# Storing ranks by halves, moving copies behind the first expert's weights, and reordering the join in a mixture-of-experts kernel

## The chip, the cores and the metric

The kernel runs on one core of one Trainium2 chip. The metric is the device time of one execution in microseconds, as the median of several runs. All data are 32-bit floats. In the text PE is TensorE, the matmul engine; DVE is VectorE, ACT is ScalarE, POOL is GpSimd and SP is SyncE, which here only issues DMAs.

## The reference

The input x holds 32 batches of 128 rows and 1024 columns. Two blocks are added to it, one after the other.

The first block mixes the 128 rows of each batch with a 128x128 matrix chosen by an index, and sends the 4096 rows that result through a mixture of 64 experts. Each row goes to its eight best experts; an expert takes at most 256 rows, in order, and rows beyond that are left out.

```
w = weights[cond]                                  # (32,128,128)
h = einsum('bct,bcd->bdt', x, w).reshape(4096, 1024)
probs = softmax(h @ gate_w.T);  w, sel = top_k(probs, 8);  w = w / w.sum()
pos  = running count of each expert's rows;  keep where pos < 256
out  = (silu(xin @ wg[e]) * (xin @ wu[e])) @ wd[e]   # xin: the 256 rows of expert e
x1   = x + sum over the 8 experts of w * out
```

The second block applies to each batch of x1 a linear map W with a low-rank correction (rank 16) of an adapter that the batch chooses, then a feed-forward map base_w with bias and a router that adds the low-rank maps of two of eight LoRA experts.

```
H   = x1 @ W.T + scal * (x1 @ A[adapter].T) @ Bm[adapter].T
y   = x1 + H @ base_w.T + base_b + 2 * sum over top-2 of gate * (H @ lora_A[e]) @ lora_B[e]
```

## The kernel before

The kernel has four stages on one core, one after the other. Times are those of the profiled execution.

Stage A, 0 to about 217 us, works on eight groups of four batches. For each group `scored` (L344) multiplies the transposed rows with the gate weights (products pxg; operands xTb and gw_sb), `logits` (L380) finds the eight best experts, and `mixed` (L362) mixes each batch (products ph) and stores the result h from ACT into the DRAM buffer `hbuf` (L373). `counted` (L410) makes two small products per half group: prk holds, for each expert and batch, the place of every row among the expert's rows and its weight. ACT copies both halves into one tile rk, and one DMA on ACT's queue stores it in the DRAM buffer `ranks` (L418). pcnt adds the counts to `upto`. `loaded_batch` (L332) loads x on SP six batches ahead. `carried` (L375) copies 512 KB of x from DRAM to the DRAM buffer `ybuf`, on SP's queue: the experts later add their outputs to ybuf. The loop over groups (L460 to L490) calls it for batch b - 8 from the ninth batch on, and the last eight copies follow the loop (L493 and L494). PE also works on products of the second block's weights meanwhile: `combined(0, d)` multiplies 388 columns of a head matrix with blocks of W (products pcw, tiles hw and WB_a), and stores them in the DRAM buffer `cwbuf`.

Between A and B, 217 to 277 us, the first search runs. `looked_up` (L214) works out on DVE in which batch each slot's row is, `fetched` (L235) gathers the rows of `ranks` for the first four experts with eight indirect DMAs on POOL (tile rkg, L242), and `found` (L253) compares and sums them on DVE (hit, byq) and multiplies byq with a constant on PE (product prow). `placed` writes the row numbers, and `gathered` (L299) fetches the rows of h on POOL (tile xin, L306). These steps are called between the halves of `combined(1, d)`: PE's order is eight products of a pcw, then prow, then the next eight.

Stage B, 277 to 2139 us, is a loop over the 64 experts. `loaded` (L555) issues the loads of wg, wu and wd on SP's queue, at 1.5 MB each. The tile of wg shares its two buffers with the head blocks hw, those of wu and wd share theirs with the blocks of W. At the end of each expert its outputs are added to ybuf by indirect DMAs on POOL (L704).

Stage C, 2139 to about 2203 us, joins the two blocks. The loop at L940 to L961 makes the last products of the head matrix, with nine steps d of eight products each (pcw<-hw,WB_b). `with_ones` (L768) adds the identity to a chunk of the map BM on DVE, for the new columns of step d. At d == 2 it does this for the other 640 columns of eight chunks, which come back from cwbuf, and `map_sums` (L750) forms four sums of them. At d == 3 `turned_x1` (L796) transposes the first pair of batches on DVE from xq into X; xq is loaded from ybuf by four DMAs on SP (`loaded_x1`, L774). At d == 4 `inner` (L805) multiplies X with the adapter maps (products px) and masks them (xm on DVE), and at d == 5 `turned_in` transposes xm on PE (products pt).

Stage D, 2203 to 2766 us, multiplies the 16 pairs of batches with the joined map (products pr_c) and stores the output.

What sets the order: the names dve, pe, act, pool and sync are wrappers (`InOrder`, L200) that keep the order of the program on their engine; all their instructions carry line L206 in the profile. Plain nc.sync and nc.gpsimd calls are placed by the scheduler. It lets an instruction pass another that waits for a buffer where no order is kept. [...]

The lines that matter for the wait of the last `ranks` store and for the join:

```
            act.dma_start(ranks[:, g * GB : (g + 1) * GB, :, :], rk_sb)
...
                if b >= 8:
                    carried(b - 8)
...
        if d == 2:
            for c in range(HC):
                with_ones(c, 0, first, BM[:, c, :, 0:first])
            map_sums(0, first)
        elif d == 3:
            X = turned_x1(0, xq, c1)
```

Of the kernel before, what the change touches and what calls it, by code (L numbers as in the profile page):

```python
# [8 lines left out]
F32 = mybir.dt.float32  # L9
# [8 lines left out]
P = 128  # L18
NB = 32
# [3 lines left out]
E = 64  # L23
# [9 lines left out]
GB = 4  # L33
# [18 lines left out]
def kernel(  # L52
# [31 lines left out]
    ybuf = dram.tile([NT + P, H], F32, name="ybuf")  # L84


    ranks = dram.tile([E, NB + 1, 2, P], F32, name="ranks")
# [38 lines left out]
    for q in range(1, NQ):  # L126
        nc.vector.tensor_scalar(over[:, q - 1 : q], pcol, float(q * Q), None, ALU.is_ge)
    nc.vector.tensor_reduce(quad, over, AX.X, ALU.add)
    inquad = const.tile([P, 1], F32, name="inquad")
# [70 lines left out]
    class InOrder:  # L200
# [7 lines left out]
    dve, pe, act, pool, sync = (  # L208
        InOrder(e) for e in (nc.vector, nc.tensor, nc.scalar, nc.gpsimd, nc.sync)
    )  # L210
# [3 lines left out]
    def looked_up(es):  # L214
# [5 lines left out]
        for j in range(NJ):  # L220
            past = fs.tile([P, n, NB], F32, name=f"past_{u}_{j}", tag="past")
            dve.tensor_scalar(past, some, slotc[:, j : j + 1], None, ALU.is_le)
            dve.tensor_reduce(batch[:, :, j], past, AX.X, ALU.add)
            dve.tensor_tensor(past, past, some, ALU.mult)
            dve.tensor_reduce(rank[:, :, j], past, AX.X, ALU.max)
            dve.tensor_scalar(
# [26 lines left out]
    def found(some, lo, hi):  # L253
# [9 lines left out]
        )  # L263
        dve.tensor_reduce(place, hit, AX.X, ALU.add)
        dve.tensor_tensor(
# [6 lines left out]
        mine = slice(u * NJ, u * NJ + n)  # L272
        dve.tensor_reduce(slot_w[:, mine], hit, AX.X, ALU.add)
        empty = fs.tile([P, n], F32, name=f"empty_{u}", tag="empty")
# [24 lines left out]
    def gathered(e):  # L299
# [15 lines left out]
            halves.append(xin)  # L315
        return halves


    with (
        tc.tile_pool(name="a1", bufs=1) as a1,  # L320
# [7 lines left out]
        def loaded_turned(b):  # L328
            xTs[b] = a6.tile([P, HC, P], F32, name=f"xTb_{b}", tag="xTb", bufs=4)
            sync.dma_start(xTs[b].rearrange("p j c -> p (j c)"), x_t[b])  # L330
# [41 lines left out]
                    dve.tensor_copy(h_sb[:, cols], ph)  # L372
            act.dma_start(hbuf[rows, :], h_sb)  # L373

        def carried(b):  # L375
            sync.dma_start(ybuf[b * P : (b + 1) * P, :], x[b])

        def logits(g, xg):  # L380
            plog = pa_sm.tile([P, GB, E], F32, name=f"plog_{g}", tag="sm")
            for t in range(GB):
                pe.matmul(plog[:, t, :], ws[g * GB + t], xg[:, t, :], start=True, stop=True)
            top = a2.tile([P, GB, K], F32, name=f"top_{g}", tag="top")
            left = a2.tile([P, GB, E], F32, name=f"left_{g}", tag="left")
            for t in range(GB):
                dve.max(top[:, t, :], plog[:, t, :])
                dve.match_replace(left[:, t, :], top[:, t, :], plog[:, t, :], LOW)
            nmax = a2.tile([P, GB], F32, name=f"nmax_{g}", tag="nmax")
            dve.tensor_scalar(nmax, top[:, :, 0], -1.0, None, ALU.mult)  # L390
            ex = a2.tile([P, GB, E], F32, name=f"ex_{g}", tag="ex")
            for t in range(GB):
                act.activation(ex[:, t, :], plog[:, t, :], AF.Exp, bias=nmax[:, t : t + 1])
            mask = a2.tile([P, GB, E], F32, name=f"mask_{g}", tag="mask")
            dve.tensor_scalar(mask, left, LOW, None, ALU.is_equal)
            return ex, mask

        def weights_of(g, ex, mask):
            wt = a2.tile([P, GB, E], F32, name=f"wt_{g}", tag="wt")
            dve.tensor_tensor(wt, ex, mask, ALU.mult)  # L400
            wsum = a2.tile([P, GB], F32, name=f"wsum_{g}", tag="wsum")
            dve.tensor_reduce(wsum, wt, AX.X, ALU.add)
            rsum = a2.tile([P, GB], F32, name=f"rsum_{g}", tag="rsum")
# [4 lines left out]


        def counted(g, mask, wt):  # L410
            rk_sb = a2.tile([E, GB, 2, P], F32, name=f"rk_{g}", tag="rk", bufs=1)
            for i in range(2):
                prk = pa_sm.tile([E, 2, 2, P], F32, name=f"prk_{g}_{i}", tag="sm")
                for t in range(2):
                    pe.matmul(prk[:, t, 0, :], mask[:, 2 * i + t, :], tri, start=True, stop=True)
                    pe.matmul(prk[:, t, 1, :], wt[:, 2 * i + t, :], ident, start=True, stop=True)
                act.copy(rk_sb[:, 2 * i : 2 * i + 2, :, :], prk)
            act.dma_start(ranks[:, g * GB : (g + 1) * GB, :, :], rk_sb)  # L418
            pcnt = pa_sm.tile([P, GB, E], F32, name=f"pcnt_{g}", tag="sm")
            pe.matmul(pcnt, ones, mask, start=True, stop=True)  # L420
            for t in range(GB):
                b = g * GB + t
                if b == 0:
                    dve.tensor_copy(upto[:, :, b], pcnt[:, t, :])
                else:
                    dve.tensor_tensor(upto[:, :, b], upto[:, :, b - 1], pcnt[:, t, :], ALU.add)
# [14 lines left out]
            yield  # L441

        gw_sb = a1.tile([P, HC, E], F32, name="gw_sb")
        loaded_turned(0)
        sync.dma_start(gw_sb.rearrange("p j e -> p (j e)"), gate_w)
        for b in range(1, GB):
            loaded_turned(b)
        for b in range(6):
# [13 lines left out]
        for g in range(NG):  # L462
            ex, mask = logits(g, xg)
            for t in range(GB):
                b = g * GB + t
                mixed(b)
                if t == 1:
                    wt = weights_of(g, ex, mask)
                if b + 6 < NB:
                    loaded_batch(b + 6)  # L470
                if b >= 8:
                    carried(b - 8)
            if g == NG - 2:
                for buf in (hbuf, ybuf):
                    act.dma_start(
                        buf[NT : NT + P, :].rearrange("p (n c) -> p n c", c=256),
                        zeros.unsqueeze(1).to_broadcast([P, H // 256, 256]),
                    )
                act.dma_start(ranks[:, NB, :, :], pad)
            for _ in range((0, 1, 1, 1, 1, 1, 2, 2)[g]):  # L480
                for _ in combined(*rest.pop(0)):
                    pass
            if g + 1 < NG:
                xg = scored(g + 1)
                if g == 0:
                    lefts += left_block("a", 1, "wd")
                    lefts += left_block("a", 2, "wu")
                if g == 4:
                    hws[1] = head_block(1)
            counted(g, mask, wt)  # L490
        part = {0: looked_up([0, 1, 2, 3])}
        fetched(part[0], 4 * NJ)
        for b in range(NB - 8, NB):  # L493
            carried(b)  # L494
        gathers = {}
        for d in range(HC + 1):
            step = combined(1, d)
# [38 lines left out]
    with (  # L536
# [18 lines left out]
        def loaded(e):  # L555
            wg_sb = wts.tile([P, HC * BW], F32, name=f"wg_{e}", tag="wg")
            nc.sync.dma_start(wg_sb[:, 0 : HC * I], wg[e])
            wg_sb = wg_sb[:, 0 : HC * I].rearrange("p (j i) -> p j i", j=HC)
            wu_sb = wts.tile([P, HC, I], F32, name=f"wu_{e}", tag="wu")
            nc.sync.dma_start(wu_sb.rearrange("p j i -> p (j i)"), wu[e])  # L560
            wd_sb = wts.tile([P, IC, H], F32, name=f"wd_{e}", tag="wd")
            nc.sync.dma_start(wd_sb.rearrange("p i h -> p (i h)"), wd[e])
            return wg_sb, wu_sb, wd_sb
# [160 lines left out]
    c1 = ctx.enter_context(tc.tile_pool(name="c1", bufs=1, reuse_waits="tile"))  # L724
# [71 lines left out]
    def turned_x1(q, xq, side):  # L796
        X = side.tile([P, KC, 2 * P], F32, name=f"X_{q}", tag="X", bufs=1)
        for t in range(2):
            dve.transpose(
                X[:, 0:HC, t * P : (t + 1) * P].rearrange("p j (q r) -> p q j r", r=Q),  # L800
                xq[:, t * NQ : (t + 1) * NQ, :].rearrange("p q (j c) -> p q j c", c=Q),
            )
        return X
# [131 lines left out]
    xq = loaded_x1(0, c1)  # L935
# [4 lines left out]
    for d in range(HC + 1):  # L940
        _, pcw = multiplied(2, d, hw, lefts, pc_p, "pp", pe)
        pcw = pcw.rearrange("p (n c) -> p n c", n=2)
        if d < HC:
            with_ones(d, first, 512, pcw)
        else:
            act.copy(BM[:, HC + 1, :, first:512], pcw)
        if d == 2:
            for c in range(HC):
                with_ones(c, 0, first, BM[:, c, :, 0:first])
            map_sums(0, first)  # L950
        elif d == 3:
            X = turned_x1(0, xq, c1)
        elif d == 4:
            pxs, xm = inner(0, X, ab)
            ab = own_maps(1)
        elif d == 5:
            turned_in(0, X, HC + 1, xm)
        elif d == 6:
            mid = routed(0, pxs, corrected(0, X, pxs))
        elif d == 7:  # L960
            turned_in(0, X, HC, mid)  # L961
# [8 lines left out]
    xq = loaded_x1(1, c3)  # L970

    for q in range(NQP):
# [21 lines left out]
        if more:  # L994
            X = turned_x1(q + 1, xq, side)
        if q + 2 < NQP:
            xq = loaded_x1(q + 2, (c1, c3)[q % 2])
# [99 lines left out]
```

## Time and profile before

| | |
|---|---|
| median of 3 runs | 2783.18 us (2773.07 to 2784.08) |
| the profiled execution, its own time | 2768.09 us |
| its span | 2766.4 us |
| PE busy | 2729.5 us, 99% of the span |
| DVE busy | 1581.5 us, 57% |
| POOL busy | 1123.1 us, 41% |
| ACT busy | 408.6 us, 15% |
| DMA | 585.11 MB, 212 GB/s in the mean |
| mean granted clock of TensorE | 0.992 |

PE's busy time by stage, from the windows view:

| stage | window, us | PE busy, us | clock | DMA busy |
|---|---|---|---|---|
| A | 0 to 217 | 204.85 | 0.95 | 96% |
| first search | 217 to 277 | 52.51 | 0.91 | 70% |
| B | 277 to 2139 | 1861.01 | | |
| C | 2139 to 2203 | 54.08 | 0.92 | 61% |
| D | 2203 to 2766.4 | 557.00 | | |

The page gives busy time per engine, then groups of instructions with the idle time ahead of them and what ended it. The list of waits gives, for one engine, the line, the operand that came last, the sum, the count and the longest wait. The timeline shows instructions in order of time; a bracket holds the idle time before one and its releaser. The windows view gives for a stretch the busy time of each engine, the granted clock (1.00 is full speed) and the share of time that the DMA engines were busy. All times count from the start of the span.

### The profile page before, as it was taken

The numbers are of one execution on the slowest core, as the hardware profiler recorded it, in microseconds if no ns is written. First come the engines' busy times: TensorE is split into PE (matmuls) and PEld (weight loads), VectorE is DVE, ScalarE is ACT, GpSimd is POOL, SyncE is SP. The second block draws the span as 40 slices with busy tenths as digits, with TensorE's granted clock in tenths as the row PEclk, the third lists the DMA queues.
The fourth block names the chain that finished last, engine by engine and source line by source line (L and its number), as shares of the span: only waits on it lengthen the run. The fifth ranks groups of instructions, "written<-read, shape, count | busy, mean of one in ns | idle before, by whom it ended". The sixth has DMA issues, their size and how long they took to land.

```text
span 2766.4 us, 23669 instructions
## 1 busy us (share of the span) xinstructions
PE 2729.5 (99%) x8580; PEld 1513.0 (55%) x8580; DVE 1581.5 (57%) x2521; ACT 408.6 (15%) x792; POOL 1123.1 (41%) x846
## 2 busy tenths in 40 slices
PE   8998999999999999999999999999999899999999
PEld 6765555555555555555555555555555555555554
DVE  2334667666676666766657667576563444444442
ACT  1220111111111111111111111111111000000000
POOL 2105365555655646556465564655451100000000
PEclk9999999999999999999999999999999999999999
DMA  9997777777878878777787777777775522222210
GB/s 349 381 376 263 238 255 227 248 262 225 251 241 243 255 225 252 256 234 248 235 249 254 229 247 253 241 244 238 237 248 153 137 74 62 62 61 65 60 43 38
DMA packets 131141, 585.11 MB, mean 212 GB/s; under 512 B 23312, under 2 KB 50000, under 8 KB 105168
## 3 DMA queue, kind: packets, MB, share of 16 engines
q1 hardware_dynamic: 71136, 405.18, 39.6%
q0 software_dynamic: 51200, 155.24, 24.3%
q10 hardware_dynamic: 8688, 23.17, 2.2%
q8 instruction: 68, 1.11, 0.2%
q14 instruction: 49, 0.40, 0.0%
HBM read 476.45 MB, written 123.83 MB: 217 GB/s over the span
## 4 chain that ended last, share of the span: by engine, by line
PE 96%; DMA 2%; DVE 1%; issue 0%; ACT 0%; SPq 0%; POOL 0%; ACTq 0%; DVEq 0%
PE pp L594 42%; PE po L693 23%; PE pr_c L206 17%; PE pcw L206 4%; PE px L206 2%; PE pxg L206 2%; PE ph L206 2%; PE pth L644 2%; DMA xTb<-in_x_t 1%; DMA hbuf<-h 1%; PE prk L206 1%; PE plog L206 0%; DMA rkg<-ranks,row 0%; PE pg L206 0%; PE pt L206 0%
## 5 line engine op out<-in xcount | busy, mean ns | idle before, releaser
L306 POOL DMA_INDIRECT xin<-hbuf,slot_row x512 | 722.6, 1411 | 159.2 <-issue 151.8
L693 PE MATMUL po<-wd,hTb 128*128 128x512 f32 x1536 | 680.3, 592 | 0.6 <-ACT hTb L646 0.6
L704 POOL DMA_INDIRECT ybuf<-o,slot_tok x128 | 205.3, 1604 | 666.1 <-ACT o L702 465.4
L693 PEld LDWEIGHTS po<-wd,hTb 128*128 128x128 f32 x1536 | 286.8, 190 | 323.7 <-issue 306.1
L594 PE MATMUL pp<-wg,xT 128*128 128x384 f32 x1024 | 351.6, 486 | 0.6 <-ACT G_sb L206 0.6
L594 PE MATMUL pp<-t,s 128*128 128x384 f32 x1024 | 341.9, 487 | 0.0
L594 PEld LDWEIGHTS pp<-t,s 128*128 128x128 f32 x1024 | 193.4, 190 | 141.9 <-issue 23.0
L206 DVE TENSOR_TENSOR u<-p,pp 128x384 f32<-128x384 f32 x64 | 35.4, 554 | 386.4 <-PE pp L594 386.4
L594 PEld LDWEIGHTS pp<-wg,xT 128*128 128x128 f32 x1024 | 189.6, 190 | 119.9 <-ACT G_sb L206 1.2
L702 ACT ACTIVATE o<-po,slot_w 128x512 f32<-128x512 f32 x256 | 175.9, 687 | 494.1 <-PE po L693 489.9
L206 POOL DMA_INDIRECT ab<-in_AT,adapter_rows x32 | 36.6, 1144 | 444.2 <-ACT pxw L206 438.9
L206 PE MATMUL pr_c<-BM,X 128*128 128x512 f32 x480 | 213.7, 592 | 0.0
L206 DVE STREAM_TRANSPOSE xT<-xin 128x1024 f32<-128x1024 f32 x128 | 156.1, 1235 | 67.6 <-DMA xin<-hbuf,slot_row 62.4
L594 PE MATMUL pp<-t,xT 128*128 128x384 f32 x512 | 175.6, 486 | 0.0
L594 PE MATMUL pp<-wu,xT 128*128 128x384 f32 x512 | 175.6, 486 | 0.0
L594 PE MATMUL pp<-wu,s 128*128 128x384 f32 x512 | 175.6, 486 | 0.0
L611 ACT ACTIVATE h<-gate 128x384 f32<-128x384 f32 x128 | 67.2, 525 | 699.6 <-DVE gate L206 699.6
L242 POOL DMA_INDIRECT rkg<-ranks,row x128 | 124.8, 975 | 96.7 <-DMA cwbuf<-cw 58.0
L206 PE MATMUL pr_c<-ts,ss 128*128 128x512 f32 x320 | 142.5, 592 | 1.3 <-DVE ss L206 1.3
L206 PEld LDWEIGHTS pr_c<-BM,X 128*128 128x128 f32 x480 | 88.9, 190 | 100.2 <-issue 100.0
L206 DVE TENSOR_TENSOR u<-u,pp 128x384 f32<-128x384 f32 x128 | 70.6, 551 | 125.0 <-PE pp L594 124.9
L594 PEld LDWEIGHTS pp<-wu,xT 128*128 128x128 f32 x512 | 97.3, 190 | 67.8
(158 smaller groups left out, 2920.4 us busy)
## 6 DMA issues: line engine op xcount, KB each, us to landing
wg<-in_wg SPq DMA_DIRECT2D x64, 1536.0 KB, 7.0
wu<-in_wu SPq DMA_DIRECT2D x64, 1536.0 KB, 9.7
wd<-in_wd SPq DMA_DIRECT2D x64, 1536.0 KB, 7.2
xTb<-in_x_t SPq DMA_DIRECT2D x32, 512.0 KB, 7.0
x<-in_x SPq DMA_DIRECT2D x32, 512.0 KB, 9.1
hbuf<-h ACTq DMA_DIRECT2D x32, 512.0 KB, 6.9
ybuf<-in_x SPq DMA_DIRECT2D x32, 512.0 KB, 8.3
xq<-ybuf SPq DMA_DIRECT2D x64, 256.0 KB, 5.1
```

The lines of the kernel that those rows point to most:

```text
L206: return lambda *args, **kw: kept(op(*args, **kw))
L242: nc.gpsimd.indirect_dma_start(out=some["rk"][:, s, :, :].rearrange("p i t -> p (i t)"), out_offset=None, in_=ranks.rearrange("e b i t -> ...
L306: nc.gpsimd.indirect_dma_start(out=xin[:, q, :], out_offset=None, in_=quarters, in_offset=bass.IndirectOffsetOnAxis(ap=slot_row[:, s : s + ...
L594: nc.tensor.matmul(bank, left[k][:, j, :], right[k][:, j, :], start=(j == 0), stop=(j == HH - 1))
L611: nc.scalar.activation(h, gate, AF.Sigmoid)
L644: nc.tensor.transpose(pt[:, i, :], h[:, i * P : (i + 1) * P], ident)
L693: nc.tensor.matmul(po, hT[j][:, i, :], wd_sb[:, i, cols], start=(i == 0), stop=(i == IC - 1),)
L702: nc.scalar.mul(o_sb[:, cols], po, slot_w[:, s : s + 1])
L704: nc.gpsimd.indirect_dma_start(out=ybuf, out_offset=bass.IndirectOffsetOnAxis(ap=slot_tok[:, s : s + 1], axis=0), in_=o_sb, in_offset=None ...
```

## The change

Five edits are made together.

- `counted` makes one tile per half group, and stores each half by its own DMA on ACT: sixteen stores of 128 KB in rows of 2 KB in place of eight of 256 KB in rows of 4 KB. The tile has two buffers instead of one.
- The load of gw_sb is issued ahead of the first xTb load instead of behind it.
- `carried` moves inside the condition on b + 6, so that the loop makes only copies 0 to 17.
- The other fourteen copies, 18 to 31, are issued in `loaded(0)`, between wu and wd of the first expert, and no longer in the loop and behind `fetched`. `carried` itself is defined further up so that it can be called there.
- In the join the two transposes of `turned_x1` are at d == 2, and the eight `with_ones` and `map_sums` at d == 3.

```diff
@@ -315,6 +315,9 @@
             halves.append(xin)
         return halves
 
+    def carried(b):
+        sync.dma_start(ybuf[b * P : (b + 1) * P, :], x[b])
+
 
     with (
         tc.tile_pool(name="a1", bufs=1) as a1,
@@ -372,9 +375,6 @@
                     dve.tensor_copy(h_sb[:, cols], ph)
             act.dma_start(hbuf[rows, :], h_sb)
 
-        def carried(b):
-            sync.dma_start(ybuf[b * P : (b + 1) * P, :], x[b])
-
 
 
         def logits(g, xg):
@@ -408,14 +408,15 @@
 
 
         def counted(g, mask, wt):
-            rk_sb = a2.tile([E, GB, 2, P], F32, name=f"rk_{g}", tag="rk", bufs=1)
             for i in range(2):
+                rk_sb = a2.tile([E, 2, 2, P], F32, name=f"rk_{g}_{i}", tag="rk")
                 prk = pa_sm.tile([E, 2, 2, P], F32, name=f"prk_{g}_{i}", tag="sm")
                 for t in range(2):
                     pe.matmul(prk[:, t, 0, :], mask[:, 2 * i + t, :], tri, start=True, stop=True)
                     pe.matmul(prk[:, t, 1, :], wt[:, 2 * i + t, :], ident, start=True, stop=True)
-                act.copy(rk_sb[:, 2 * i : 2 * i + 2, :, :], prk)
-            act.dma_start(ranks[:, g * GB : (g + 1) * GB, :, :], rk_sb)
+                act.copy(rk_sb, prk)
+                two = slice(g * GB + 2 * i, g * GB + 2 * i + 2)
+                act.dma_start(ranks[:, two, :, :], rk_sb)
             pcnt = pa_sm.tile([P, GB, E], F32, name=f"pcnt_{g}", tag="sm")
             pe.matmul(pcnt, ones, mask, start=True, stop=True)
             for t in range(GB):
@@ -441,8 +442,8 @@
             yield
 
         gw_sb = a1.tile([P, HC, E], F32, name="gw_sb")
+        sync.dma_start(gw_sb.rearrange("p j e -> p (j e)"), gate_w)
         loaded_turned(0)
-        sync.dma_start(gw_sb.rearrange("p j e -> p (j e)"), gate_w)
         for b in range(1, GB):
             loaded_turned(b)
         for b in range(6):
@@ -468,8 +469,8 @@
                     wt = weights_of(g, ex, mask)
                 if b + 6 < NB:
                     loaded_batch(b + 6)
-                if b >= 8:
-                    carried(b - 8)
+                    if b >= 8:
+                        carried(b - 8)
             if g == NG - 2:
                 for buf in (hbuf, ybuf):
                     act.dma_start(
@@ -490,8 +491,6 @@
             counted(g, mask, wt)
         part = {0: looked_up([0, 1, 2, 3])}
         fetched(part[0], 4 * NJ)
-        for b in range(NB - 8, NB):
-            carried(b)
         gathers = {}
         for d in range(HC + 1):
             step = combined(1, d)
@@ -558,6 +557,9 @@
             wg_sb = wg_sb[:, 0 : HC * I].rearrange("p (j i) -> p j i", j=HC)
             wu_sb = wts.tile([P, HC, I], F32, name=f"wu_{e}", tag="wu")
             nc.sync.dma_start(wu_sb.rearrange("p j i -> p (j i)"), wu[e])
+            if e == 0:
+                for b in range(NB - 14, NB):
+                    carried(b)
             wd_sb = wts.tile([P, IC, H], F32, name=f"wd_{e}", tag="wd")
             nc.sync.dma_start(wd_sb.rearrange("p i h -> p (i h)"), wd[e])
             return wg_sb, wu_sb, wd_sb
@@ -945,11 +947,11 @@
         else:
             act.copy(BM[:, HC + 1, :, first:512], pcw)
         if d == 2:
+            X = turned_x1(0, xq, c1)
+        elif d == 3:
             for c in range(HC):
                 with_ones(c, 0, first, BM[:, c, :, 0:first])
             map_sums(0, first)
-        elif d == 3:
-            X = turned_x1(0, xq, c1)
         elif d == 4:
             pxs, xm = inner(0, X, ab)
             ab = own_maps(1)
```

In the programs as built, PE's order of instructions is the same as before. On DVE only the join differs. On SP wu of the first expert goes ahead with eight of the fourteen copies, then wg, the other six copies and wd follow.

## The prediction

> **What bounds the kernel now.** I read the page first, then all waits of TensorE, then the timeline around each wait that the change touches, then the windows with the granted clock.
>
> ```profile
> PE 2729.5 (99%) x8580; PEld 1513.0 (55%) x8580; DVE 1581.5 (57%) x2521; ACT 408.6 (15%) x792; POOL 1123.1 (41%) x846
> ```
>
> TensorE is busy 2729.5 of 2766.4 us. The matmul order stays the same in the built programs, so only two things can be won: the 36.9 us in which PE idles, and the time it runs at half clock because of such idling. The list of PE's waits (total, count, longest) splits the idle time:
>
> ```profile
> PE px L206 <- issue: 9.9, 1, 9.9
> PE prow L206 <- DVE byq L206: 7.0, 1, 7.0
> PE pxg L206 <- DMA gw_sb<-in_gate_w: 6.5, 1, 6.5
> PE pxg L206 <- DMA xTb<-in_x_t: 3.4, 7, 1.4
> ```
>
> The change aims at the first three: the join (px), the first row search (prow) and the start (gw_sb). The prow chain in the timeline (start, busy, instruction, in brackets the idle time before it and its releaser):
>
> ```profile
> 218.27 0.58 ACT L206 COPY rk<-prk 64x512 f32<-64x512 f32 x1 [0.29 <-PE prk L206]
> 222.92 0.45 ACTq L206 DMA_DIRECT2D ranks<-rk  x1
> 226.91 0.95 POOL L242 DMA_INDIRECT rkg<-ranks,row  x1 [58.00 <-DMA cwbuf<-cw]
> ...
> 235.90 0.42 DVE L206 TENSOR_TENSOR hit<-rkg,rank 128x256 f32<-128x256 f32 x1 [12.78 <-DMA rkg<-ranks,row]
> ...
> 238.94 0.59 PE L206 MATMUL prow<-byq,spread 128*128 128x8 f32 x2 [7.04 <-DVE byq L206]
> 239.38 8.05 PE L206 MATMUL pcw<-hw,WB_a 128*128 128x388 f32 x16
> 247.41 5.46 PE L206 MATMUL pcw<-hw,WB_a 128*128 128x388 f32 x16
> ```
>
> The last ranks store is issued at 222.92, although its data is ready at 218.85: 4.07 us late. Each DMA of SP and ACT uses one of eight completion semaphores in turn and waits for the DMA that last used it. Here that was the hbuf store of 207.88, in flight for 15.0 us among the x copies (the three before it: 4.2 to 4.6). After prow, sixteen pcw take 8.05 us, later ones 5.46. The windows view says why (window, length, PE, PEld, DVE, ACT, POOL, clock, DMA, GB/s):
>
> ```profile
> 224.14:234.38 10.24, 7.75 (x24) 4.18 (x22) 0.00 (x0) 0.93 (x2) 5.69 (x6) 1.00 0.79 277
> 234.38:244.62 10.24, 5.68 (x10) 3.29 (x11) 5.99 (x21) 0.00 (x0) 5.54 (x6) 0.50 0.63 232
> 2169.73:2179.97 10.24, 4.64 (x18) 4.67 (x19) 7.12 (x7) 0.00 (x0) 0.00 (x0) 0.50 0.23 51
> ```
>
> An idle stretch is followed by 10.24 us at clock 0.50, here and at the join. Two more such spells stand at 60.30 and 186.59. The join in DVE's and PE's timeline:
>
> ```profile
> 2159.95 6.45 DVE L206 SCALAR_TENSOR_TENSOR BM<-chan,own,BM 128x640 f32<-128x640 f32 x8 [4.22 <-DMA BM<-cwbuf]
> ...
> 2173.46 0.61 DVE L206 SCALAR_TENSOR_TENSOR BM<-chan,own,pcw 128x384 f32<-128x384 f32 x1
> 2173.99 2.36 DVE L206 STREAM_TRANSPOSE X<-xq 128x1024 f32<-128x1024 f32 x2
> 2175.32 6.65 PE L206 MATMUL px<-pxw,X 128*128 128x152 f32 x32 [9.92 <-issue]
> ```
>
> and the last of the four loads of xq, which the transposes read (issued 2156.92, so landed 2170.2):
>
> ```profile
> L778 SPq DMA_DIRECT2D xq<-ybuf x1: 474/474/474, 2156.9 to 2156.9; - x1
> DMA to landing us min/median/max: 13.3/13.3/13.3
> ```
>
> "issue" hides that px waits for the transposes, and they behind 13.4 us of ones and sums on DVE (2159.95 to 2173.4).
>
> [...]
>
> **The change part by part.** All sums are against the profiled execution (span 2766.4 plus 1.69 around it, 2768.09), which is 15.1 us under the median of 2783.18; I move the median by the same amount.
>
> *gate_w first.* PE's first pxg needs gw_sb (landed 6.39) and xTb_0 (5.72). The same 768 KB go through one queue in either order. Cost 0, between -0.3 and +0.3: the 0.67 us between the landings, halved.
>
> *Ranks in halves, copies behind wu_0.* Eight more ACT issues of 0.45 us: ACT is busy 408.6 us in all, so they lie beside PE. In the built program SP runs on to wu_0 right behind copy 17 and the three small loads (about 193 us), then eight copies, then wg_0, six copies, wd_0: wg_0's buffer is released only by the first block's last product (216.3), so the scheduler lets wu_0 and eight copies pass. These are 5.5 MB between 193 and 216, where now fifteen copies (7.5 MB) are issued from 191 to 216. So the queue is nearly empty when the ranks come; the last half waits for the semaphore of the fourth copy, which waits for wu_0's landing (about 201) and lands near 210. The half is issued when its data is there, 219.1 instead of 222.92; behind it on ACT are only copies of later pcw, with four buffers between them and PE. But wg_0 (1.5 MB) and four copies (2 MB) start at 216.5: at about 400 GB/s (369 GB/s is the mean of 0 to 217 us, DMA 96% busy) they fill the queues to about 226.5, and the last two copies to 229. The half's landing takes 3.2 us (now, alone) to 7.6 (ranks of group 6 at 198.17, beside copies); I take 5: 224.1, gathers rkg from 224.9 (now 226.91). The second is issued at 226.2. Now the first two take 7.1 and 7.6 us beside wg_0 and wu_0; the shortest gathers in the trace take 2.6 to 2.8. I take its landing at 231.0, two us after the copies have drained; 3.3 us on through hit to prow (235.78 to 238.94 now, rounded up) gives 234.3. PE is ready at 231.9, so it waits 2.4 instead of 7.04: -4.6. [...] the half-clock spell still comes, and PE now has work in nearly all of it instead of 5.7 us; half of the extra 4.6 is lost: +2.3. Net **-2.3 us**. Bounds: -9.9 if the wait and the spell go (7.04 and half of 5.68; gathers at 2.8 us would do it); +0.4 with the half at 7.6 and the gathers at 7.6. Behind the waiting gathers on POOL only the xin gathers are queued, and their products have 8 us of slack: token sums end at 268.95, the first product is at 277.13.
>
> *Earlier groups.* Loop copies 18 to 23 leave a stretch that is DMA-bound, but only one xTb wait and no x wait sits there; 0, with 5.1 either way for a half-clock spell more or less (that is what those at 60 and 187 cost).
>
> *The join.* Two transposes move ahead of one pcw ones, eight ones and four sums. They can't start before xq lands at 2170.26; the change starts no xq load earlier. So DVE stands from 2155.7 to 2170.3[...]. PE: px from about 2171.5, at half clock to 2179.97, done about 2180.0; pcw 5 done 2185.3. DVE: 2170.3 + 2.3 (transposes) + 14.0 (3 x 0.6 less overlap, eight ones 6.45, four sums 7.2) = 2186.5, then 0.5 for with_ones(4): xm at 2187.0, its transposes on PE at 2187.75 against 2186.97 now: **+0.8 us**. The 9.9 us before px becomes about 6.1, and a new wait of 2.4 us stands behind pcw 5. That second gap may start another half-clock spell, up to +4.9 us; I take 0. The cover of the sums is gone: they lay beside the xq load.
>
> Sum: -2.3 + 0.8 = -1.5, 2766.6 for the profiled execution, **2781.7** for the median.
>
> **The rivals.**
> A. The join gains in full: xq lands by about 2160, say because the scatter adds or cwbuf drain earlier. Then px's 9.92 us and the 2.35 lost at half clock (6.65 against 4.30 for the same matmuls later) go: -12.3, with prow -2.3: -14.6, 2768.6. For it: DMA is idle enough after 2164. Against: 13.3 us to landing, queued behind BM's 2.5 MB. Chance 0.12. With C, -22.2 or 2761.0: 0.07.
> B. Slower: each group now holds two semaphores with ranks stores, and in the built program xTb_16/17, 20/21 and 24/25 wait on halves of groups 2 to 4; only xTb_17, 21 and 25 waited before. xTb_20 to 23 landed at 127.84 to 136.02 with PE needing them about 2 us apart, waiting 0.17 to 0.27 each: no reserve. A delay of half a microsecond per group plus a half-clock spell of 5.1 is 5.6; three groups give 16.8 - 1.5 = +15.3, 2798.5. It decides from three groups (two: 11.2 - 1.5 = +9.7, 2792.9, within the bound). Against: halves are stored earlier than the whole. Chance 0.10.
> C. The prow wait goes wholly, with its spell: -9.9 + 0.8 = -9.1, 2774.1. For it: 2 MB less ahead, and gathers of 2.8 us elsewhere. Against: wg_0 and six copies run beside the ranks and the gathers. Chance 0.15.
> D. The change doesn't do what its words say: wu_0 and eight of fourteen copies are ahead of wg_0; this is in the forecast.
>
> **How the numbers follow.** Forecast 0.56, A 0.12, A with C 0.07, B 0.10, C 0.15. A measurement of this kernel can tell about 0.5%, 13.9 us. Faster: A and A with C, with 0.01 for the tail of C, 0.20. Slower: B, 0.10. Same: 0.70. Range: low 2766.3, A with prow's full -4.6; high 2792.9, two groups of B. A with C and B stay outside, 0.17. The forecast's own range is 2774.1 (prow's lower bound) to 2789.3 (prow +0.4 instead of -2.3, and a spell in the second gap of the join, 4.9).
>
> **What the changed profile would show.** px waits about 6 instead of 9.9 us, DVE idle up to the transposes for xq, and pt (xm) 48.3 us after the join's first pcw (47.5 now); prow waits about 2.4 us; the last ranks half is issued near 219 and lands near 224, beside wg_0; four half-clock spells remain. I'm wrong if xq lands before 2165, if the last half is issued after 221 or prow doesn't wait, or if groups 4 to 6 show xTb waits of over half a microsecond.

## The result and the profile after

| | before | after |
|---|---|---|
| median of 22 runs each | 2783.31 us | 2788.77 us |
| ratio of after to before | | 1.0029, 95% interval 1.0016 to 1.0041 |
| the profiled execution: span | 2766.4 us | 2789.4 us |
| mean granted clock of TensorE | 0.992 | 0.988 |

The changed kernel is slower by 0.29%, about 8 us: the ratio is that of the means, which lie 8.0 us apart; the medians lie 5.5 us apart. That is less than the 0.5% that the prediction set as the bound of what can be told; 22 runs of each tell it. The two profiled executions differ by 23.0 us, since the one of before lies at the low end of its kernel's runs and the one of after close to its median. So where an argument rests on a size, several profiles are put side by side below. The 23.0 us lie in three places: 8.6 up to the end of stage A, 10.2 from there to the first product of the experts, and 4.2 from there to pg, the product that follows pt in the join. From pg to the end both take 574.0 us.

The list of PE's waits after the change (total, times, longest):

```profile
PE prow L206 <- DVE byq L206: 17.1, 2, 11.9
PE pxg L206 <- DMA xTb<-in_x_t: 11.3, 8, 6.5
PE px L206 <- issue: 7.2, 1, 7.2
PE pt L206 <- DVE xm L206: 4.1, 1, 4.1
```

The px wait has fallen from 9.9 to 7.2 us, and a wait for xm before pt has come in its place. The prow wait has grown from 7.0 to 17.1, in two waits of 11.9 and 5.2. The xTb wait now holds the 6.5 us of the start (gw_sb no longer lands last); the rest, 4.8 us, lies in the groups, where before had 3.4.

Beside the waits stands the clock. The granted clock in 1 us steps shows these half-clock spells. The last two columns give the end of PE's last product of stage A (prk) and the end of ACT's last copy to rk, which is called the end of stage A here:

| kernel | ranks stored | half-clock spells up to 205 us | sum, us | last product, us | end of stage A, us |
|---|---|---|---|---|---|
| before | whole, ACT | 60-71, 186-197 | 20.4 | 218.2 | 218.9 |
| before, second profile | whole, ACT | none | 0 | 210.1 | 210.7 |
| after | halves, ACT | 59-70, 110-124, 168-172, 199-203 | 30.7 | 223.5 | 227.4 |
| after, second profile | halves, ACT | 60-74, 115-126, 197-204 | 30.6 | 224.1 | 227.4 |

The start of group 4's operands in the timeline, before and then after (start, busy, instruction):

```profile
92.58 9.22 SPq L206 DMA_DIRECT2D xTb<-in_x_t  x4
94.14 0.46 ACTq L206 DMA_DIRECT2D ranks<-rk  x1
```

```profile
92.37 0.46 ACTq L206 DMA_DIRECT2D ranks<-rk  x1
93.48 0.45 ACTq L206 DMA_DIRECT2D ranks<-rk  x1
98.90 4.15 SPq L206 DMA_DIRECT2D xTb<-in_x_t  x4
...
108.92 2.49 PE L206 MATMUL pxg<-gw_sb,xTb 128*128 128x64 f32 x16 [0.70 <-DMA xTb<-in_x_t]
112.86 7.09 PE L206 MATMUL pxg<-gw_sb,xTb 128*128 128x64 f32 x32 [1.46 <-DMA xTb<-in_x_t]
```

Before, the first of the four xTb loads goes out at 92.58, ahead of the ranks store. After, it has to wait for the semaphore that the first ranks half holds (4.2 us in the list of SP's waits), and goes out at 98.90. PE then waits 0.70 us, and half clock begins at 110.3; the wait of 1.46 us falls into it. Behind that, 32 of these products take 7.09 us, where 64 took 7.25 at full clock.

Each DMA in a trace names its completion semaphore, so one can read which DMA used it last. In the trace of before the 465 DMAs of SP and ACT name eight of them, 58 or 59 DMAs each, and each of the 457 that use one again goes out after the DMA that used it last has landed: the xTb loads of 92.58 and 99.98 by 0.06 us, the ranks store of 222.92 by 0.07. The first xTb load of groups 4, 5 and 6, counted from 0:

| kernel | issued, us | its semaphore was last used by |
|---|---|---|
| before | 92.58, 118.83, 141.81 | a copy to ybuf |
| after | 98.90, 125.14, 150.65 | the first ranks half |
| halves alone, ACT | 98.77, 123.24, 149.29 | the first ranks half |
| halves alone, POOL | 92.80, 116.58, 140.67 | a load of x |
| quarters, ACT | 102.27, 129.32, 156.29 | a load of x; the copy to ybuf just ahead of it on SP waits for a ranks store |

The second load of these groups waits for a ranks store before the change too (99.98 for group 4).

The prow chain after the change:

```profile
223.15 0.38 PE L206 MATMUL prk<-ident,wt 128*64 128x128 f32 x2
223.37 0.58 ACT L206 COPY rk<-prk 64x512 f32<-64x512 f32 x1
226.35 0.45 ACTq L206 DMA_DIRECT2D ranks<-rk  x1
226.84 0.58 ACT L206 COPY rk<-prk 64x512 f32<-64x512 f32 x1 [2.90 <-DMA hbuf<-h]
227.45 0.45 ACTq L206 DMA_DIRECT2D ranks<-rk  x1
240.34 0.94 POOL L242 DMA_INDIRECT rkg<-ranks,row  x1 [62.21 <-DMA ybuf<-in_x]
...
249.10 0.60 PE L206 MATMUL prow<-byq,spread 128*128 128x8 f32 x2 [11.90 <-DVE byq L206]
```

The last half goes out 0.03 us after its copy has ended (227.42), but that copy is itself late. The first half is ready at 223.95 and its store waits until 226.35 for the semaphore of the hbuf store of 220.44; the second copy stands behind it on ACT (the bracket: 2.90 us). From the last product to the last store it takes 3.9 us, against 4.7 before (217.85 + 0.38 to 222.92):

```profile
217.85 0.38 PE L206 MATMUL prk<-ident,wt 128*64 128x128 f32 x2
```

The gathers start only 12.9 us after the store: it is in flight beside wg_0 and the six copies behind it. And the join after the change, DVE and PE:

```profile
2189.76 2.37 DVE L206 STREAM_TRANSPOSE X<-xq 128x1024 f32<-128x1024 f32 x2 [15.51 <-DMA xq<-ybuf]
...
2192.55 6.45 DVE L206 SCALAR_TENSOR_TENSOR BM<-chan,own,BM 128x640 f32<-128x640 f32 x8
...
2206.57 0.42 DVE L206 TENSOR_TENSOR xm<-px,smask 128x256 f32<-128x256 f32 x1
```

```profile
2191.11 6.67 PE L206 MATMUL px<-pxw,X 128*128 128x152 f32 x32 [7.19 <-issue]
...
2207.05 0.69 PE L206 MATMUL pt<-ident,xm 128*128 128x128 f32 x2 [4.11 <-DVE xm L206]
2207.53 7.97 PE L206 MATMUL pcw<-hw,WB_b 128*128 128x384 f32 x16
```

DVE stands 15.51 us until xq has landed, and only then makes the ones and sums. The sixteen pcw behind pt take 7.97 us instead of 5.33: a second half-clock spell.

### The profile page after: what moved, and what is told of

Same layout as the page of the kernel before. It is cut to its first block, busy times and chain, and to the rows that moved or that the text cites. A ratio compares the mean times of both kernels' runs of the same rounds, so it can differ in the third digit from the quotient of the medians.

```text
span 2789.4 us, 23677 instructions
## 1 busy us (share of the span) xinstructions
PE 2739.2 (98%) x8580; PEld 1519.4 (54%) x8580; DVE 1580.3 (57%) x2521; ACT 408.1 (15%) x792; POOL 1119.4 (40%) x846
## 4 chain that ended last, share of the span: by engine, by line
PE 93%; DMA 4%; DVE 1%; issue 0%; POOL 0%; ACT 0%; SPq 0%; ACTq 0%; DVEq 0%
PE pp L596 41%; PE po L695 23%; PE pr_c L206 17%; PE pcw L206 3%; PE px L206 2%; PE pxg L206 2%; DMA xTb<-in_x_t 2%; PE pth L646 1%; PE ph L206 1%; DMA hbuf<-h 1%; PE prk L206 1%; DMA ybuf<-in_x 1%; DMA xq<-ybuf 0%; DMA ranks<-rk 0%; DMA cwbuf<-cw 0%
```

## The experiments

The ratios are to the kernel before, run on the same chip in the same rounds, each with its 95% interval. A diff is to the kernel before, or to the experiment that its text names.

**Each part alone.** The join alone:

```diff
         if d == 2:
+            X = turned_x1(0, xq, c1)
+        elif d == 3:
             for c in range(HC):
                 with_ones(c, 0, first, BM[:, c, :, 0:first])
             map_sums(0, first)
-        elif d == 3:
-            X = turned_x1(0, xq, c1)
```

> Only the reordering of the join is made (transposes at d == 2, ones and sums at d == 3). Theory 1 (the transposes still wait for xq, so the ones and sums lose the cover of that load): the px wait falls from 9.9 us by some 3, a new wait of about 4 us stands before pt of xm, and the kernel is 2 to 5 us slower than before (ratio 1.001 to 1.002). Rival (the join pays by itself, what is lost is lost at the first search and in the groups): 5 to 12 us faster, ratio 0.996 to 0.998.

Measured: 1.0007 (0.9984 to 1.0030), which can't tell either sign. In its profile px waits 6.5 us and pt 4.6; from the first product of the experts to pg of the join the kernel has lost 3.0 us against before. In after it is 4.2, in the second profile of after 2.2, with whole ranks (below) 3.9. So the join alone costs 2 to 4 us in four profiles, and the rival, a gain of 5 to 12, is out. (This stretch differs by up to 1.7 us between the profiles whose join is as before.)

The copies alone, fourteen of them behind wu of the first expert:

```diff
-                if b >= 8:
-                    carried(b - 8)
+                    if b >= 8:
+                        carried(b - 8)
...
-        for b in range(NB - 8, NB):
-            carried(b)
...
             nc.sync.dma_start(wu_sb.rearrange("p j i -> p (j i)"), wu[e])
+            if e == 0:
+                for b in range(NB - 14, NB):
+                    carried(b)
```

> Only the copies are moved (18 to 31 behind the first expert's wu); ranks are stored whole. Theory 1 (the copies behind wg_0 now run beside the last ranks store and the gathers, which crowds both): the prow waits sum to 12 to 18 us instead of 7.0, and the kernel is 4 to 10 us slower. Rival (the halves of the ranks are what delays, through the two completion semaphores they hold): no slower than before, prow waits under 7 us.

Measured: 1.0015 (0.9994 to 1.0036), prow wait 12.9 us. The time leaves it open whether the copies cost anything.

The halves alone:

```diff
-            rk_sb = a2.tile([E, GB, 2, P], F32, name=f"rk_{g}", tag="rk", bufs=1)
             for i in range(2):
+                rk_sb = a2.tile([E, 2, 2, P], F32, name=f"rk_{g}_{i}", tag="rk")
...
-                act.copy(rk_sb[:, 2 * i : 2 * i + 2, :, :], prk)
-            act.dma_start(ranks[:, g * GB : (g + 1) * GB, :, :], rk_sb)
+                act.copy(rk_sb, prk)
+                two = slice(g * GB + 2 * i, g * GB + 2 * i + 2)
+                act.dma_start(ranks[:, two, :, :], rk_sb)
```

> Only the ranks are stored by halves. Theory 1 (the copies are at fault): within 2 us of before, prow wait near 7 us, xTb waits as before. Rival (halves hold two semaphores and delay the xTb loads of groups 4 to 6): xTb waits of 1 us or more in these groups, half-clock spells behind them, 5 us or more slower.

Measured: 1.0028 (1.0010 to 1.0046), as much as the whole change. Stage A ends at 226.1 us, with half-clock spells at 87-94, 134-149 and 196-203. My first theory, that the copies are at fault, falls here. This profile also shows what SP's wait can do to the DMA engines. The windows view (last three columns: clock, share of time that the DMA engines were busy, GB/s):

```profile
95.00:98.00 3.00, 3.00 (x15) 1.92 (x14) 2.49 (x14) 0.35 (x1) 0.00 (x0) 1.00 0.73 285
98.00:101.00 3.00, 3.00 (x8) 1.24 (x7) 2.52 (x9) 1.99 (x6) 1.89 (x2) 1.00 0.35 74
```

The xTb loads go out at 98.77, behind the landing of a half that was issued at 94.27; until then the queues run low, in a stage in which the DMA engines are otherwise 94% busy. It isn't so each time: in the two profiles of after the engines are fully busy from 98 to 101 us (1.02 and 0.98).

The kernel before, for a second profile:

> The kernel before, unchanged, for a second profile. Its profiled execution was 15 us under its own median, so a second one shows where a usual execution spends those 15 us. Theory 1: the excess lies in stage A and in the first search (xTb waits, prow wait, half-clock spells); the join and the stages of the experts and of the output agree within 1 us. Rival: it is spread over all stages with the clock.

It took 2764.0 us, again at the low end, so it can't show where a usual execution spends its 15 us more; that stays open. It does show how far two such executions differ inside: no half-clock spell in stage A (20.4 us of them in the first), 8.2 us less to the end of stage A, but a prow wait of 12.1 us instead of 7.0. Two other profiles, those of the join alone and of the join with xq first, show one place where a good part of it can lie, where their edits change nothing: between 260 and 290 us the last 72 pcw ahead of the experts take 35.5 and 39.1 us instead of 23.7, with gaps of up to 2.0 us that the trace puts down to no releaser ("issue"). No run tests the cause.

**What the halves cost.** The halves alone, stored from POOL, so that none of the eight semaphores of SP and ACT is held: 457 DMAs use them instead of 473 (diff to the halves alone):

```diff
-                act.dma_start(ranks[:, two, :, :], rk_sb)
+                pool.dma_start(ranks[:, two, :, :], rk_sb)
```

> Ranks by halves in the same two tiles and with the same rows of 2 KB, but stored from POOL, so that they take none of the eight completion semaphores of SP and ACT. Semaphore theory (the halves cost because loads on SP wait until a ranks store that held their semaphore has landed): the 8 us of the halves on ACT are gone, ratio 0.997 to 1.001, stage A ends about 8 us earlier than with the halves on ACT. Rival (more and smaller stores, or the second tile, cost by themselves): 1.002 to 1.004 as with the halves on ACT.

Measured: 0.9978 (0.9964 to 0.9992). Stage A ends at 218.4 us. Tile, rows and number of stores are as with the halves on ACT; the queue and the semaphores are what differs, and this run can't tell the two apart. Its one profile has still 23.9 us at half clock in stage A (27.3 with the halves alone on ACT), but PE waits 3.3 us there after its first product instead of 7.6; the gain is read from the 22 runs.

The halves alone, with two stores for each half, four in a group (diff to the halves alone):

```diff
-                act.dma_start(ranks[:, two, :, :], rk_sb)
+                for t in range(2):
+                    act.dma_start(ranks[:, g * GB + 2 * i + t, :, :], rk_sb[:, t, :, :])
```

> Ranks in half tiles, but each half stored by two DMAs on ACT, one for each batch: four stores in a group, which hold four semaphores. Semaphore theory: more loads on SP wait for a store, so the cost of the halves (0.28%) grows, ratio 1.004 to 1.008, and stage A is longer by another 5 us or more. Rival (the cost is that of splitting the tile, not of semaphores): 1.002 to 1.004 as with halves.

Measured: 1.0076 (1.0050 to 1.0102). Stage A ends at 239.2 us, with spells at 60-74, 115-129 and 169-180; xTb waits 9 times, 7.7 us in all. Both expectations of the semaphore theory hold in size, and the table of the xTb loads shows the way: SP keeps its order, so a copy that waits for a ranks store holds the load behind it: that of group 4 goes out at 102.27 instead of 92.58. Some 8 us of the end of stage A are no time of PE: its last product ends at 230.8, and the last copy stands behind the first half's stores on ACT. The rows of these stores are 1 KB instead of 2; what that costs was not measured apart.

The changed kernel with whole ranks, the copies and the join as changed (diff to the changed kernel):

```diff
+            rk_sb = a2.tile([E, GB, 2, P], F32, name=f"rk_{g}", tag="rk", bufs=1)
             for i in range(2):
-                rk_sb = a2.tile([E, 2, 2, P], F32, name=f"rk_{g}_{i}", tag="rk")
...
-                act.dma_start(ranks[:, two, :, :], rk_sb)
+            act.dma_start(ranks[:, g * GB : (g + 1) * GB, :, :], rk_sb)
```

> The changed kernel with the ranks stored whole again (one tile, one store a group); copies, gw_sb and the join as changed. If the halves are the main cost of the change: ratio to before 0.999 to 1.002, stage A (to the end of the last rk copy) near 218 us instead of 227. Rival (the copies and the join carry the loss, the halves only add to it by chance): 1.002 to 1.004.

Measured: 1.0002 (0.9987 to 1.0016). Stage A ends at 215.9 us. Without the halves the rest of the change makes no difference that can be told.

**What the copies cost.** All fourteen copies behind wd of the first expert, ranks whole (diff to the copies alone):

```diff
             nc.sync.dma_start(wu_sb.rearrange("p j i -> p (j i)"), wu[e])
-            if e == 0:
-                for b in range(NB - 14, NB):
-                    carried(b)
             wd_sb = wts.tile([P, IC, H], F32, name=f"wd_{e}", tag="wd")
             nc.sync.dma_start(wd_sb.rearrange("p i h -> p (i h)"), wd[e])
+            if e == 0:
+                for b in range(NB - 14, NB):
+                    carried(b)
```

> Only the copies are moved, but all fourteen behind wd of the first expert instead of between wu and wd; ranks whole, join as before. Crowding theory (copies issued around the last ranks store make it land late): from the last ranks store to the first gather about 4 us instead of the 9.3 with copies behind wu, the first prow waits under 7 us; time 0.997 to 1.001, unless the gathers of h, which now run beside the copies, take back what is won. Rival (the store is late for another reason): 9 us from store to gather again, prow wait above 10.

Measured: 0.9971 (0.9957 to 0.9984). Its timeline:

```profile
218.82 0.45 ACTq L206 DMA_DIRECT2D ranks<-rk  x1
224.45 0.94 POOL L242 DMA_INDIRECT rkg<-ranks,row  x1 [55.06 <-DMA ranks<-rk]
...
228.46 0.43 DVE L206 TENSOR_TENSOR hit<-rkg,rank 128x256 f32<-128x256 f32 x1 [5.39 <-DMA rkg<-ranks,row]
```

The whole store, 256 KB, goes out at once and is there for the gathers 5.6 us later (4 were expected); hit follows 4.0 us after the first gather instead of 9.0. The first prow doesn't wait. What comes back later, as was allowed for: the third prow waits 7.7 us, and the first product of the experts 6.1.

**What the join costs.** xq's loads ahead of BM, WB_b and lora_B, with the join as changed (diff to the join alone):

```diff
+    xq = loaded_x1(0, c1)
     at = NX
     for lo, hi in PIECES[0:2]:
...
-    xq = loaded_x1(0, c1)
```

> The join reordered as in the change, and the four loads of the first xq issued ahead of the loads of BM, the last left block and lora_B, which need the same last scatter. Landing theory (the swap fails only because xq lands at the end of a 7 MB queue): xq lands about 12 us earlier, px waits 0 to 2 us, no half-clock spell at the join; the join is 10 to 15 us shorter than before, ratio 0.995 to 0.997. Rival (DVE's own work at the join is the bound): px still waits over 5 us or pt of xm takes the wait, within 4 us of before.

Measured: 0.9986 (0.9974 to 0.9997), a third of what was expected. px no longer waits: from the first product of the experts to the end of px 12.7 us are gained. But 6.1 are lost before pt, which waits 6.0 us for xm, and 2.3 behind it at half clock; 4.3 us remain. The landing theory is right on px, and its rival on pt. So the four sums were put behind xm as well (diff to the kernel just told):

```diff
                 with_ones(c, 0, first, BM[:, c, :, 0:first])
-            map_sums(0, first)
         elif d == 4:
             pxs, xm = inner(0, X, ab)
             ab = own_maps(1)
+            map_sums(0, first)
```

> As the join with xq loaded first, but the four sums are put behind xm: transposes at d == 2, the eight ones at d == 3, the sums behind inner at d == 4. Theory (with xq early the px wait goes, and the rest of the gain was lost because DVE makes 7.2 us of sums and 6.5 us of ones ahead of xm): pt of xm no longer waits 6 us, the join is 12 us shorter than before from its first product to pg, no half-clock spell in it, ratio 0.994 to 0.997. Rival (the sums then delay the router's DVE work at d == 6, and the wait only moves again): a new wait of 4 us or more at pt of mid or behind it, ratio 0.998 or above.

Measured: 0.9938 (0.9914 to 0.9962). The join, shown by PE's timeline, has no wait and no half clock:

```profile
2160.65 4.30 PE L206 MATMUL px<-pxw,X 128*128 128x152 f32 x32
2164.79 5.32 PE L206 MATMUL pcw<-hw,WB_b 128*128 128x384 f32 x16
2169.95 0.38 PE L206 MATMUL pt<-ident,xm 128*128 128x128 f32 x2
```

From the first product of the experts to pg it is 12.0 us shorter than before. The ratio makes 17 us of it, but its interval, from 8 runs, reaches from 11 to 24; that there is more than the join in it is not shown.

**The mended parts together:** halves from POOL, copies behind wd, the join with xq first and the sums behind xm.

> Three mended parts together: halves stored from POOL, the fourteen copies behind wd of the first expert, the join with xq first and the sums behind xm. If the parts add (0.22%, 0.29% and some 0.4%): ratio 0.989 to 0.993, no wait before the first prow, none over 2 us before px and pt. Rival (the gains at the first search exclude each other, since both shorten the same wait): 0.993 to 0.996.

Measured: 0.9917 (0.9893 to 0.9941), median 2755.0 us against 2781.4: faster than both kernels. No wait is left before the first prow, px and pt; the third prow waits 5.6 us. The product of the three ratios is 0.9887; it lies just outside the interval, and whether the parts add in full can't be told, since each of them has its own.

The changed kernel, for a second profile:

> The changed kernel, unchanged, for a second profile. If the account holds: end of the last rk copy at 223 to 230 us, the last ranks store issued within 1 us of it, 8 us or more from store to first gather, prow waits over 10 us in all, px wait 6 to 8 us and pt wait about 4 us with two shorter half-clock spells in the join.

It took 2787.1 us. Stage A ends at 227.4, the last half goes out 0.03 us after its copy, the gathers start 12.4 us later, prow waits 16.6 us in all, px 6.6 and pt 3.9, with spells of 6.8 and 3.4 us in the join. All within what was expected.

## Why the prediction was wrong, point by point

The forecast was -1.5 us; the change costs 0.29%, about 8 us. What happened is rival B, to which I gave one chance in ten, at less than the 9.7 us that I took for two groups. The median after, 2788.77, lies inside the forecast's own range, but that is luck: the upper end of that range was made of a lost gain at prow and a spell in the join, with nothing for the groups.

*Earlier groups, taken as 0: this step failed.* It looked at the copies that leave the loop and not at the semaphores. The end of PE's last product of stage A sorts the twelve kernels and their fourteen profiles by where and in how many pieces the ranks are stored. Whole on ACT: 209.2 to 218.2 us, mean 214.5 of eight profiles. Halves on ACT: 223.5, 223.7, 224.1. Quarters: 230.8. Halves from POOL: 217.7 and, in the mended kernel, 209.0; the first of these lies inside the range of whole ranks, so it is the runs (0.9978) that show the cost to be gone.

So the halves cost 223.8 - 214.5 = 9.3 us in the profiles, and 0.28% by themselves, 7.8 us. Of the 9.3, 7.7 are time in which PE is busy longer and 1.7 are waiting (0.1 comes off at the start). The sum of half-clock time in stage A is 29.5 us in the mean with halves and 11.9 with whole ranks; half of the difference, my estimate of what it costs, is 8.8 us, which is enough for the longer busy time. The end of stage A, the last copy to rk, is 11.8 us later (227.0 against 215.2): the other 2.5 us are the last copy's wait on ACT behind the first half's store. B's price (half a microsecond of delay and a spell of 5.1 us per group) was of the right kind.

Against B I had put that halves are stored earlier than the whole. The first half is, in group 4's turn 1.7 us behind the first prk for 2.6; the second, at 2.9, is not. And two DMAs move the turn of every semaphore behind them, and the first xTb load of a group comes to wait for a store that is issued at about the time at which SP comes to that load (92.37 and 94.65 for group 4). It is this place in the turn that counts and not the sum of SP's waits for ranks stores: up to 215 us that is 25.6 to 32.3 us in three profiles with whole ranks, 32.9 to 34.6 with halves and 22.9 with quarters.

*Ranks in halves, at the first search, taken as -2.3: wrong.* The last half was to be issued when its data is there, and to land 5 us later. It goes out when its copy ends, but the step had overlooked the first half, whose store waits for a semaphore of its own and holds that copy. Nor is the queue nearly empty when the ranks come: in the profile of the copies alone wu_0 goes out at 199.44 and not near 193, and the eight copies from 200.46 to 217.85, up to wg_0. From the last product of stage A to the first gather:

| kernel | product to last store | store to gather | sum, us |
|---|---|---|---|
| five profiles with stage A as before | 4.7 to 11.8 | 4.0 to 7.3 | 8.7 to 15.8, mean 13.2 |
| copies behind wu, ranks whole (two kernels) | 4.5, 5.2 | 9.3, 8.7 | 13.9, 13.9 |
| halves, copies as before | 2.6 | 7.8 | 10.5 |
| halves from POOL, copies as before | 0.9 | 7.3 | 8.2 |
| after (two profiles) | 3.9, 3.3 | 12.9, 12.4 | 16.8, 15.7 |
| copies behind wd, ranks whole | 0.7 | 5.6 | 6.3 |

The halves take a part of the delay before the store away; the copies, which now run beside it, give back more than that as flight time. The two rows of whole ranks with moved copies show that it's the place of the copies that lengthens the flight, since nothing that bears on the store differs between them but that place. My own bound for the landing, 7.6 us, was taken from a store among the copies of the loop and was too small. After the change 128 KB take 12.9 us to the first gather beside wg_0 and six copies on SP's queue; the share of wg_0 in it was not measured apart. That the half-clock spell would still come there, as counted in the +2.3, was my estimate; after the change one of 13.65 us begins at 239.96, before one of 10.24 at 234.38. I had also built this step on one profile, in which prow waits 7.0 us; in four others of the same code up to there it is 11.6 to 14.4.

*gate_w first, taken as 0: right.* The first pxg starts at 6.51 after and 6.53 before.

*The join, taken as +0.8: right in mechanism, too small.* The transposes wait for xq as was said; pt stands 49.1 us after the first pcw of the join (48.3 forecast, 47.5 before). The term that was mis-sized is the spell in the second gap, taken as 0 of a possible 4.9: the gap is 4.1 us instead of 2.4, the spell comes, and it adds 1.4 to 2.9 us from pt to pg, in after and in three other profiles. Together 2 to 4 us. Rival A (xq in time) is out: the two transposes start 31.8 us after the join's first pcw, and xq landed 30.8 us after it before.

*Rival C (no wait at the first prow)* happened only with the copies behind wd. *D* held: wu_0 and eight copies pass wg_0.

## What to carry to other kernels

Splitting a store in two was not free here, where the DMAs of SP and ACT share eight completion semaphores: the halves alone took 1.0028 of the time of before, and 0.9978 when stored from POOL's queue. Ask which load comes up next behind each half, and whether it may wait. In stage A, where the DMA engines are 94% busy after the change, a wait of PE of 0.70 us was followed by 13.7 us at half clock, in which PE is busy for 12.2 and so loses about 6, by estimate. It isn't always so: the second profile of before has six such waits, the longest 0.9 us, and no spell in stage A. When an engine issues DMAs in order, look also at what stands behind one that waits: here the last copy to rk stood 2.90 us on ACT behind the first half's store. When a wait moves, follow the next two instructions behind it: the reordered join paid only when its load and the sums behind it were moved too.

## What was not expected of the hardware

The half-clock spells are not all of 10.24 us. In the profile of after they last 3.41 us (from 168.28), 6.83 (from 267.26), 10.24 (from 59.05) and 13.65 (from 110.25), one to four times 3.41. PE was busy for all 10.24 us of the third and for 12.19 us of the fourth. A ranks half of 128 KB took 12.9 us to the first gather beside copies, a whole store of 256 KB 5.6 us without them.
